# Reading the scan's decay from PSUM and forming the gate's product on GpSimd

## The chip, the cores and the metric

The kernel runs on one NeuronCore of a Trainium2 chip, in one launch. The metric is the device time of one execution in microseconds (us); the time of a kernel is the median of its runs. The core has five engines that each work through their own queue in order: TensorE (PE, matrix products into PSUM), VectorE (DVE), ScalarE (ACT), GpSimd (POOL) and SyncE (SP, which issues most DMAs). They wait for each other through semaphores.

## What is computed

Four residual layers work on 32 images of 192 channels and 56 x 56 pixels: agent attention, a bidirectional RWKV scan, a shifted depthwise 3 x 3 filter and a long convolution done through spectra. Each begins with a group norm. The change touches the second layer alone. With `xs` the normed images as 3136 pixels of 192 channels:

```python
k, v, r = xs @ Wk.T, xs @ Wv.T, xs @ Wr.T
real_w = -exp(w_decay)                       # one number per channel
x_fwd = wkv_scan(real_w, u, k, v)            # running sums over the pixels
x_bwd = flip(wkv_scan(real_w, u, flip(k), flip(v)))
h = sigmoid(r) * 0.5 * (x_fwd + x_bwd)
h = layernorm(h) * ln_g + ln_b               # over the channels
out = x + h @ Wo.T
```

`wkv_scan` keeps a numerator and a denominator per channel, multiplies both by `exp(real_w)` at every pixel and adds `exp(k) * v` and `exp(k)`; the present pixel enters with the weight `exp(u)`; the quotient is the result. The kernel keeps the two sums without the running maximum (a guarded version, `scan_guarded`, is there for inputs that need it, and is not entered here).

## The kernel before

`all_blocks` runs four stages one after another: `make_filter`, `attention`, `scan_pairs`, `channel_blocks`. The change is in `scan_pairs`.

**Tiles.** Two images are worked on at once, as a pair; there are 16 pairs. The 2 x 192 channels of a pair fill three tiles of 128 partitions: tile 0 holds channels 0 to 127 of the first image, tile 1 those of the second, and tile 2, the third tile, the remaining 64 of both. The 3136 pixels go in four pieces of 784 (`MC`), so an elementwise instruction is 128 x 784, and a matrix product fills two PSUM banks with 392 columns each (`HM`).

**Products.** `turned()` (L925) gives a PSUM tile of two banks out of a pool of four, which is all of PSUM (eight banks). Products for tiles 0 and 1 are made together by `_Pairs.outer` (L886 to L893): four matmuls of L890, then four of L893, into two PSUM tiles. Products for the third tile are made by `_Pairs.inner` (L895 to L903): two matmuls of L900, then four of L903, into one. The profile records each matmul twice, so a pair of tiles shows as 8 and 8, a third tile as 4 and 8.

**One step.** The loop at the end of `scan_pairs` runs over pairs and pieces. A full step does, for three different places in the data: `backwards` (the backward scan of one piece), `finish` (layer norm, output product and residual of the piece that `backwards` ended a step earlier), and `forwards` (the forward scan of a piece of the next pair). There are 60 full steps, four forward-only pieces ahead of them, and four steps without `forwards` at the end.

The lines of a step, by name:

- `normed` (L1110): ACT applies the group norm to the loaded `x`.
- `forwards`: the product with `Wk`; ACT takes the exponential, `ek` (L1159); the product with `Wv`; DVE multiplies it by `ek`, giving `bv` (L1164); then `scan`, `inverse` and `y = p * q` on DVE (L1174).
- `scan` (L1113 to L1132), once for `bv` (giving `p`) and once for `ek` (giving `q`): POOL copies the carry into the edge column (L1123), DVE runs the scan (L1128), POOL copies the last column out as the next carry (L1129), DVE adds the present pixel with its weight (L1130). Carries are named f and b for forward and backward, with 0 for p or 1 for q, and the tile: f11 is the forward carry of q in tile 1.
- `inverse` (L1135, L1136): ACT inverts the denominator through Ln and Exp.
- `backwards`: the product with `Wr`; ACT makes the gate `g` in three instructions (L1188, L1192, L1193); the scans; on DVE the quotient (L1196), its sum with the forward result (L1197) and the product with the gate (L1198).
- `finish`: the product of `h` with a centring matrix; ACT squares it (L1213); the mean over channels of the squares, a product for tiles 0 and 1 alone (two PSUM tiles, from `mean_w`); ACT forms the reciprocal deviation through Ln and Exp (L1222, L1223); two DMAs on ACT's queue bring it into the third tile's layout; the output product with `wog`; DVE scales it (L1236) and adds it to the image (L1239); ACT squares that for the next group norm (L1246).

**What sets the order.** The source order is only the input of a scheduler that runs when the program is built. It simulates the engines with costs of its own and picks, for every engine, a fixed order, and it places the waits. It treats two accesses of different engines to the same PSUM tile as ordered when they share a bank, whether or not they share columns. On the chip each engine takes its queue in that order.

The lines that a sentence does not say:

```python
def turned():
    ps = pp.tile([128, 2, BANK], F32, name="ps", tag="ps")
    return ps, ps[:, :, :HM], [ps[:, h, :HM] for h in range(2)]
...
nc.vector.tensor_tensor_scan(out, decay[:, of(t)].to_broadcast([128, MC]), data, at, ALU.mult, ALU.add)
nc.gpsimd.tensor_copy(at, z[:, last : last + 1])
nc.vector.scalar_tensor_tensor(before, src, c, before, ALU.mult, ALU.add)
```

`decay` is a tile of two columns in SBUF: one for tiles 0 and 1, one for the third. The scan reads one of them with step zero, 784 times.

Of the kernel before, what the change touches and what calls it, by code (L numbers as in the profile page):

```python
# [20 lines left out]
F32 = mybir.dt.float32  # L21
I32 = mybir.dt.int32
AF = mybir.ActivationFunctionType
ALU = mybir.AluOpType
AX = mybir.AxisListType
PSUM = bass.MemoryType.PSUM
# [10 lines left out]
MC = 784  # L37
NM = N // MC
HM = MC // 2
# [26 lines left out]
BANK = 512  # L66
# [840 lines left out]
def scan_pairs(ctx: ExitStack, tc: tile.TileContext, a, k, x1, st_a, st_c, x2, rs2, count):  # L907
# [5 lines left out]
    nc = tc.nc  # L913
# [2 lines left out]
    kp = ctx.enter_context(tc.tile_pool(name="s_k", bufs=3 * NM))  # L916
    wp = ctx.enter_context(tc.tile_pool(name="s_w", bufs=9))
    sp = ctx.enter_context(tc.tile_pool(name="s_s", bufs=2))
    pp = ctx.enter_context(tc.tile_pool(name="s_p", bufs=4, space=PSUM))
    pairs = _Pairs(nc)  # L920

    def small(name, shape):
        return cp.tile(shape, F32, name=name, tag=name)

    def turned():  # L925
        ps = pp.tile([128, 2, BANK], F32, name="ps", tag="ps")
        return ps, ps[:, :, :HM], [ps[:, h, :HM] for h in range(2)]

    def parts(t):
        return [t[:, h * HM : (h + 1) * HM] for h in range(2)]  # L930
# [21 lines left out]
    ps, _, _ = turned()  # L952
# [22 lines left out]
    decay, near, far = small("decay", [128, 2]), small("near", [128, 2]), small("far", [128, 2])  # L975
# [13 lines left out]
    nc.vector.tensor_tensor(near, near, z, ALU.mult)  # L989
    nc.vector.tensor_tensor(decay, near, far, ALU.add)  # L990

    eps = small("eps", [128, 1])
    nc.vector.memset(eps, 4.0 * LN_EPS)
    kept_a, kept_c = small("kept_a", [128, 2, NB // 2]), small("kept_c", [128, NB // 2])
# [5 lines left out]
    def of(t):  # L1000
        return slice(0, 1) if t < 2 else slice(1, 2)
# [111 lines left out]
    def scan(s, m, t, carry, rev):  # L1113

        b, e = s.bv[m][t], s.ek[m][t]
        c = eu[:, of(t)]
        got = []
        for i, src in enumerate((b, e)):
            z = wp.tile([128, MC + 1], F32, name="pq"[i], tag="pq", bufs=5)
            edge, last = (MC, 0) if rev else (0, MC)  # L1120
            out, before = (z[:, 0:MC], z[:, 1:]) if rev else (z[:, 1:], z[:, 0:MC])
            at = carry[t][i]
            nc.gpsimd.tensor_copy(z[:, edge : edge + 1], at)  # L1123
            if rev:
                out, data = out[:, ::-1], src[:, ::-1]
            else:
                data = src[:, :]
            nc.vector.tensor_tensor_scan(out, decay[:, of(t)].to_broadcast([128, MC]), data, at, ALU.mult, ALU.add)  # L1128
            nc.gpsimd.tensor_copy(at, z[:, last : last + 1])  # L1129
            nc.vector.scalar_tensor_tensor(before, src, c, before, ALU.mult, ALU.add)  # L1130
            got.append(before)
        return got  # L1132
# [12 lines left out]
    def forwards(s, m, behind=()):  # L1145
        s.ek[m] = [kp.tile([128, MC], F32, name="ek", tag="ek", bufs=3 * NM + 1) for _ in range(3)]
        s.bv[m] = [kp.tile([128, MC], F32, name="bv", tag="bv") for _ in range(3)]
        s.y[m] = [kp.tile([128, MC], F32, name="y", tag="y", bufs=3 * NM + 4) for _ in range(3)]
        xn = normed(s, m)
        for tiles in ((0, 1), (2,)):  # L1150
            for wt in (wk, wv):
                ps = [turned() for _ in tiles]
                if len(tiles) == 2:
                    pairs.outer(wt, [q[2] for q in ps], xn)
                else:
                    pairs.inner(wt, ps[0][2], xn)
                for t, (_, both, _) in zip(tiles, ps):
                    if wt is wk:
                        nc.scalar.activation(  # L1159
                            s.ek[m][t].rearrange("p (h n) -> p h n", h=2), both, AF.Exp,  # L1160
                            accum_out=s.seen[:, 0, 3 * m + t : 3 * m + t + 1],
                        )
                    else:
                        nc.vector.tensor_tensor(  # L1164
                            s.bv[m][t].rearrange("p (h n) -> p h n", h=2), both,
                            s.ek[m][t].rearrange("p (h n) -> p h n", h=2), ALU.mult,
                        )
                if wt is wk and tiles == (0, 1):
                    for later in behind:
                        later()  # L1170
            for t in tiles:
                num, den = scan(s, m, t, s.fore, False)
                inverse(s, den, m, t, 1)
                nc.vector.tensor_tensor(s.y[m][t], num, den, ALU.mult)  # L1174

    def backwards(s, m):

        xn = normed(s, m)
        h = s.y[m]
        for tiles in ((0, 1), (2,)):  # L1180
            ps = [turned() for _ in tiles]
            if len(tiles) == 2:
                pairs.outer(wr, [q[2] for q in ps], xn)
            else:
                pairs.inner(wr, ps[0][2], xn)
            for t, (_, both, _) in zip(tiles, ps):
                g = wp.tile([128, MC], F32, name="g", tag="t")
                nc.scalar.activation(  # L1188
                    g.rearrange("p (h n) -> p h n", h=2), both, AF.Exp, scale=-1.0,
                    accum_out=s.seen[:, 3, 3 * m + t : 3 * m + t + 1],  # L1190
                )
                nc.scalar.activation(g, g, AF.Ln, bias=1.0)  # L1192
                nc.scalar.activation(g, g, AF.Exp, scale=-1.0)  # L1193
                num, den = scan(s, m, t, s.back, True)
                inverse(s, den, m, t, 2)
                nc.vector.tensor_tensor(num, num, den, ALU.mult)  # L1196
                nc.vector.tensor_tensor(h[t], h[t], num, ALU.add)  # L1197
                nc.vector.tensor_tensor(h[t], h[t], g, ALU.mult)  # L1198
            yield

    def finish(s, m):

        h, xs = s.y[m], load(s.p, m)
        hs = [parts(t) for t in h]
        sq = [wp.tile([128, MC], F32, name="sq", tag="t") for _ in range(3)]
        for tiles in ((0, 1), (2,)):
            ps = [turned() for _ in tiles]
            if len(tiles) == 2:
                pairs.outer(centre, [q[2] for q in ps], hs)
            else:  # L1210
                pairs.inner(centre, ps[0][2], hs)
            for t, (_, both, _) in zip(tiles, ps):
                nc.scalar.activation(  # L1213
                    sq[t].rearrange("p (h n) -> p h n", h=2), both, AF.Square,
                    accum_out=s.seen[:, 4, 3 * m + t : 3 * m + t + 1],
                )
        sqs = [parts(t) for t in sq]
        pv = [turned() for _ in range(2)]
        pairs.outer(mean_w, [q[2] for q in pv], sqs)
        rds = [wp.tile([128, MC], F32, name="rd", tag="t") for _ in range(3)]  # L1220
        for t, (_, both, _) in enumerate(pv):
            nc.scalar.activation(rds[t].rearrange("p (h n) -> p h n", h=2), both, AF.Ln, bias=eps)  # L1222
            nc.scalar.activation(rds[t], rds[t], AF.Exp, scale=-0.5)  # L1223

        for t, r in enumerate((slice(0, 64), slice(64, 128))):
            nc.scalar.dma_start(out=rds[2][r], in_=rds[t][r])
        yield
        left = []
        for tiles in ((0, 1), (2,)):
            po = [turned() for _ in tiles]  # L1230
            if len(tiles) == 2:
                pairs.outer(wog, [q[2] for q in po], hs)
            else:
                pairs.inner(wog, po[0][2], hs)
            for t, (_, out, _) in zip(tiles, po):
                nc.vector.tensor_tensor(  # L1236
                    sq[t].rearrange("p (h n) -> p h n", h=2), out, rds[t].rearrange("p (h n) -> p h n", h=2), ALU.mult
                )
                nc.vector.scalar_tensor_tensor(  # L1239
                    xs[t], sq[t], cb[:, of(t)], xs[t], ALU.add, ALU.add, accum_out=s.sums[:, t, m : m + 1]  # L1240
                )
                if m == NM - 1:
                    nc.vector.tensor_scalar(s.away[:, t], s.sums[:, t, m : m + 1], -1.0 / MC, None, ALU.mult)

                def square(t=t):
                    nc.scalar.activation(  # L1246
                        sq[t], xs[t], AF.Square, bias=s.away[:, t], accum_out=s.squares[:, t, m : m + 1]
                    )

                left.append(square)  # L1250
        rows = slice(m * MC // S, (m + 1) * MC // S)
        for r, t, i, c in places:
            nc.sync.dma_start(out=x2[c, i, rows, s.p], in_=xs[t][r].rearrange("p (h w) -> p h w", w=S))
        yield left
# [19 lines left out]
    for m in range(NM):  # L1274
        forwards(s, m)
# [45 lines left out]
    ps, _, _ = turned()  # L1321
# [608 lines left out]
```

## Time and profile before

| What | Value |
|---|---|
| runs | 12221.74, 12241.55, 12216.5 us; median 12221.74 us |
| profiled execution, its own time | 12216.98 us |
| span of its trace | 12215.1 us |
| mean granted TensorE clock | 0.958 |
| busy over the span | PE 90%, DVE 88%, ACT 59%, POOL 28% |
| `scan_pairs`, from the first scan on | about 4997 to 8390 us, 3393 us |

The profile is of one execution. Times in a trace count from the start of its span; the execution's own time is 1.9 us more than the span. A line of a group names the source line, the engine, the operation, the tiles written and read, the shapes, how often it ran, its busy time in all, the mean of one in ns, and the engine's idle time just before it with what ended that. In a timeline the first two columns are the start and the time taken (a merged row covers several instructions), and an idle time stands in brackets. The instructions of an engine overlap a little at their ends, so the pitch from start to start is shorter than the duration.

### The profile page before, as it was taken

To read this page: it belongs to the slowest core of one execution; us is meant where nothing else is said; L and a number is where in the kernel's file an instruction comes from. 1 tells how busy PE (TensorE), PEld (TensorE's weight loads), DVE (VectorE), ACT (ScalarE), POOL (GpSimd) and SP (SyncE) were. 2 spreads that over 40 slices of the span, in tenths; PEclk is the share of its full clock that TensorE was granted. 3 is DMA by queue.
4 is the path that set the end of the run, shared out by engine and by line. 5 is a ranking of instruction groups with operands and counts; after the bars stand their busy time and mean duration, and the time that the engine had idled before them with its cause. 6 is when DMAs were issued, how large, how long until landed. Compare 5 with 4: busy or idle time off the path is not lost. (4 is left out here: it accounts for less than half of the span.)

```text
span 12215.1 us, 157485 instructions
## 1 busy us (share of the span) xinstructions
PE 11030.6 (90%) x57358; PEld 6623.6 (54%) x57358; DVE 10753.1 (88%) x14722; ACT 7146.9 (59%) x14690; POOL 3400.5 (28%) x2568
## 2 busy tenths in 40 slices
PE   6999999999999999688888888886999999999999
PEld 3555555555555555333333333333666666666666
DVE  6888888888888888799999999996888899898897
ACT  3555555555555555466666666665666666666665
POOL 0000000000000000455555555555343343343330
PEclk9999999999999999899999999997999999999999
DMA  2222222222222222243334334334333333333331
GB/s 70 57 57 57 59 58 64 59 59 59 63 61 57 57 57 49 73 103 96 97 101 104 93 97 104 98 96 100 71 68 64 67 70 64 67 70 64 67 69 32
DMA packets 1959211, 876.56 MB, mean 72 GB/s; under 512 B 1821153, under 2 KB 1858292, under 8 KB 1949292
## 3 DMA queue, kind: packets, MB, share of 16 engines
q1 hardware_dynamic: 1948188, 840.69, 30.1%
q10 hardware_dynamic: 10240, 25.70, 0.8%
q8 instruction: 458, 7.50, 0.3%
q14 instruction: 325, 2.66, 0.1%
HBM read 482.13 MB, written 319.29 MB: 66 GB/s over the span
## 5 line engine op out<-in xcount | busy, mean ns | idle before, releaser
L619 DVE SCALAR_TENSOR_TENSOR o<-v_a,att_w,o 128x896 f32<-128x896 f32 (+1 forms) x1024 | 1056.8, 1032 | 467.3 <-ACT v_a L593 337.3
L1142 POOL MEMSET f<- 128x1 f32 x96 | 8.9, 99 | 4769.6 <-DMA st_c<-st 4764.6
L1793 ACT COPY y<-ps 64x252 f32<-64x252 f32 (+1 forms) x2376 | 808.7, 340 | 797.3 <-PE ps L1787 767.6
L1626 POOL TENSOR_TENSOR smooth<-smooth,more 114x896 f32<-114x896 f32 x384 | 866.3, 2259 | 1200.7 <-ACT more L1625 1141.2
L1709 PE MATMUL ps<-fixed,real 84*84 84x112 f32 x6144 | 1093.6, 260 | 0.0
L1709 PE MATMUL ps<-fixed,imag 84*84 84x112 f32 x6144 | 1091.1, 259 | 0.0
L1717 ACT ACTIVATE z<-ps,rs 84x112 f32<-84x112 f32 x3072 | 816.7, 355 | 322.1 <-PE ps L1709 319.5
L1709 PEld LDWEIGHTS ps<-fixed,real 84*84 84x84 f32 x6144 | 790.2, 154 | 158.4 <-issue 129.4
L1135 ACT ACTIVATE q<-q 128x784 f32<-128x784 f32 x384 | 328.5, 855 | 812.4 <-DVE q L1130 641.2
L1709 PEld LDWEIGHTS ps<-fixed,imag 84*84 84x84 f32 x6144 | 765.8, 153 | 0.0
L890 PE MATMUL ps<-sq,fixed 128*128 128x392 f32 x512 | 298.9, 746 | 425.9 <-ACT sq L1213 425.9
L636 ACT ACTIVATE pr<-ps,low 98x896 f32<-98x896 f32 (+1 forms) x384 | 352.3, 918 | 559.9 <-DVE low L634 559.9
L724 PE MATMUL ps<-gq_a,xs_a 128*112 128x294 f32 x1792 | 619.1, 427 | 45.7 <-DVE pq L729 45.7
L1787 PE MATMUL ps<-fixed,padded 114*128 114x168 f32 x3072 | 527.6, 322 | 134.6 <-DVE x L1729 118.3
L619 DVE SCALAR_TENSOR_TENSOR o<-v_c,att_w,o 128x448 f32<-128x448 f32 (+1 forms) x1024 | 638.3, 623 | 6.0 <-ACT v_c L604 0.9
L632 PE MATMUL ps<-xs_a,gk_a 128*98 128x448 f32 (+1 forms) x1536 | 637.1, 495 | 0.0
L633 PE MATMUL ps<-xs_c,gk_c 125*98 125x448 f32 (+1 forms) x1536 | 631.6, 492 | 0.0
L1728 PE MATMUL ps<-z,fixed 84*114 84x448 f32 x1536 | 609.7, 539 | 0.4 <-ACT z L1717 0.4
L725 PE MATMUL ps<-gq_c,xs_c 125*112 125x294 f32 x1792 | 608.3, 421 | 0.0
L890 PE MATMUL ps<-x,weights 128*128 128x392 f32 x1536 | 574.0, 517 | 31.1 <-DVE bv L1164 14.2
L737 ACT ACTIVATE pq<-pq 112x1176 f32<-112x1176 f32 x224 | 265.4, 1185 | 553.0 <-DVE pq L729 430.1
L1787 PEld LDWEIGHTS ps<-fixed,padded 114*128 114x128 f32 x3072 | 473.6, 198 | 206.1 <-DVE x L1729 140.5
(372 smaller groups left out, 29249.8 us busy)
## 6 DMA issues: line engine op xcount, KB each, us to landing
x<-x SPq DMA_DIRECT2D x576, 392.0 KB
x<-x SPq DMA_DIRECT2D x512, 196.0 KB
x<-zeros SPq DMA_DIRECT2D x192, 399.0 KB
shifted<-x SPq DMA_DIRECT2D x192, 399.0 KB
x<-x SPq DMA_DIRECT2D x192, 399.0 KB
out_x<-x SPq DMA_DIRECT2D x384, 196.0 KB
x<-in_x SPq DMA_DIRECT2D x32, 1568.0 KB
x<-x SPq DMA_DIRECT2D x32, 1568.0 KB
```

What stands on the lines that cost most here:

```text
L619: nc.vector.scalar_tensor_tensor(dst, tap(i), dww[:, t, i : i + 1], dst, ALU.mult, ALU.add)
L632: mm(ps[P2, h, :n], g[:, cols], xs_a[j][:, px], start=True, stop=False)
L633: mm(ps[P2, h, :n], gk_c[0:KC, 2 * j + h, cols], xs_c[j][0:KC, px], start=False, stop=True)
L724: mm(ps[:SUB, i, :HA], xs_a[j][:, px], g, start=True, stop=False)
L725: mm(ps[:SUB, i, :HA], xs_c[j][0:KC, px], gq_c[0:KC, 2 * j + (q + i) // ns], start=False, stop=True)
L890: mm(out, aa, srcs[t][h], start=True, stop=False)
L1626: nc.gpsimd.tensor_tensor(y, y, more, ALU.add)
L1709: nc.tensor.matmul(ps[:84, i * 2 * S : (i + 1) * 2 * S], part[:, i0 + i].rearrange("p s u -> p (s u)"), f3[:, m, :], start=(m == 0), stop= ...
L1717: nc.scalar.activation(z[:, i0 + i].rearrange("p m w -> p (m w)"), ps[:84, i * 2 * S : (i + 1) * 2 * S], AF.Copy, scale=q.rs[:, i0 + i : i ...
L1728: nc.tensor.matmul(got, f4[:, m, :], z[:, i0 : i0 + n, m, :], start=(m == 0), stop=(m == 1))
L1787: nc.tensor.matmul(ps[:, g * 168 : (g + 1) * 168], flat[:, (g0 + g) * 128 : (g0 + g + 1) * 128], f1, start=True, stop=True)
L1793: nc.scalar.copy(y[64 * m : 64 * m + 64, 2 * g0 + i : 2 * (g0 + n) : 2], got[64 * i : 64 * i + 64, :, :, m, :])
```

## The change

A PSUM tile `own` of two banks is taken once and kept. All products for the third tile go there; the products for tiles 0 and 1 share the remaining three. The two columns of the decay are copied once into columns 392 and 393 of the first bank of `own`, behind the 392 that the products fill, and every scan reads them there. The product with the gate moves from DVE to POOL.

```diff
-    pp = ctx.enter_context(tc.tile_pool(name="s_p", bufs=4, space=PSUM))
+    pp = ctx.enter_context(tc.tile_pool(name="s_p", bufs=3, space=PSUM))
+    own = pp.tile([128, 2, BANK], F32, name="own", tag="own", bufs=1)
...
-    def turned():
-        ps = pp.tile([128, 2, BANK], F32, name="ps", tag="ps")
+    def turned(third=False):
+        ps = own if third else pp.tile([128, 2, BANK], F32, name="ps", tag="ps")
         return ps, ps[:, :, :HM], [ps[:, h, :HM] for h in range(2)]
...
+    pace = own[:, 0, HM : HM + 2]
+    nc.vector.tensor_copy(pace, decay)
...
-            nc.vector.tensor_tensor_scan(out, decay[:, of(t)].to_broadcast([128, MC]), data, at, ALU.mult, ALU.add)
+            nc.vector.tensor_tensor_scan(out, pace[:, of(t)].to_broadcast([128, MC]), data, at, ALU.mult, ALU.add)
...
-                ps = [turned() for _ in tiles]
+                ps = [turned(t == 2) for t in tiles]
...
-                nc.vector.tensor_tensor(h[t], h[t], g, ALU.mult)
+                nc.gpsimd.tensor_tensor(h[t], h[t], g, ALU.mult)
```

The edit of `turned(t == 2)` is made in `forwards`, `backwards` and twice in `finish`, so five products of a full step use `own`: those with `Wk`, `Wv`, `Wr`, the centring matrix and `wog`. In the changed file lines up to 920 keep their numbers; in `scan` and below they are higher by 5 (L1128 becomes L1133, L1198 becomes L1203).

More of the change, by code (lines that the diff above doesn't have):

```diff
@@ L1180, in backwards @@
         for tiles in ((0, 1), (2,)):
-            ps = [turned() for _ in tiles]
+            ps = [turned(t == 2) for t in tiles]
             if len(tiles) == 2:
@@ L1206, in finish @@
         for tiles in ((0, 1), (2,)):
-            ps = [turned() for _ in tiles]
+            ps = [turned(t == 2) for t in tiles]
             if len(tiles) == 2:
@@ L1229, in finish @@
         for tiles in ((0, 1), (2,)):
-            po = [turned() for _ in tiles]
+            po = [turned(t == 2) for t in tiles]
             if len(tiles) == 2:
```

## The prediction

> **What bounds the kernel now.** First the busy time of the scan stage (columns: stretch, length, PE, PEld, DVE, ACT, POOL, granted clock, DMA share, GB/s):
>
> ```profile
> 5083.00:8390.00 3307.00, 2745.99 (x10011) 1252.04 (x10011) 3217.21 (x3316) 2113.54 (x3631) 1941.04 (x1649) 0.92 0.39 98
> ```
>
> DVE is busy 3217 of 3307 us: it bounds this stage, and its 90 us of idle time make 1.4 us in each of 64 steps. A full step lasts 53.2 us (mean distance of the first L1196 of a step to the next one's), so DVE's work is 51.8. PE has 17% to spare. Second, the groups of the stage:
>
> ```profile
> L1129 POOL COPY f<-p 128x1 f32<-128x1 f32 x192 | 405.7, 2113 | 313.3 <-DVE p L1128 305.4
> ...
> L1128 DVE TENSOR_TENSOR_SCAN p<-decay,b,bv 128x784 f32<-128x784 f32 x192 | 354.6, 1847 | 0.0
> ...
> L1198 DVE TENSOR_TENSOR y<-y,g 128x784 f32<-128x784 f32 x191 | 183.4, 961 | 0.0
> ...
> L1164 DVE TENSOR_TENSOR bv<-ps,ek 128x784 f32<-128x784 f32 x192 | 180.6, 967 | 1.2 <-PE ps L893 1.2
> L1174 DVE TENSOR_TENSOR y<-p,q 128x784 f32<-128x784 f32 x192 | 180.2, 965 | 0.0
> ```
>
> L1198 is what leaves DVE. A copy of one column on POOL takes 2113 ns beside scans: it waits for DVE to let go. Third, timelines for pitches, of DVE, then of PE, and of PE after a pause (start, time, engine, line):
>
> ```profile
> 6491.14 3.60 DVE L1128 TENSOR_TENSOR_SCAN q<-decay,f,ek 128x784 f32<-128x784 f32 x2
> 6494.65 1.96 DVE L1130 SCALAR_TENSOR_TENSOR q<-ek,eu,q 128x784 f32<-128x784 f32 x2
> 6496.52 1.85 DVE L1164 TENSOR_TENSOR bv<-ps,ek 128x784 f32<-128x784 f32 x2
> 6498.29 3.59 DVE L1128 TENSOR_TENSOR_SCAN p<-decay,f,bv 128x784 f32<-128x784 f32 x2
> ```
> ```profile
> 6489.20 2.90 PE L890 MATMUL ps<-x,weights 128*128 128x392 f32 x8
> 6492.03 1.59 PE L893 MATMUL ps<-x,weights 64*128 64x392 f32 x8
> 6493.55 1.58 PE L900 MATMUL ps<-x,weights 128*128 128x392 f32 x4
> 6495.06 1.54 PE L903 MATMUL ps<-x,weights 128*64 128x392 f32 x8
> ```
> ```profile
> 5508.33 4.83 PE L890 MATMUL ps<-sq,fixed 128*128 128x392 f32 x8 [8.83 <-ACT sq L1213]
> 5513.09 1.59 PE L893 MATMUL ps<-sq,fixed 64*128 64x392 f32 x8
> ```
>
> From start to start a scan takes 1.76 us, L1130 0.94, a plain product 0.885, L1239 with its accumulator 1.03. On PE four L890 take 2.83, four L893 1.52, and a third tile's product 3.05 from its first start to its last end (the 302 such groups of the stage: median 3.051). After 8.83 us of idling the same four L890 take 4.76. I sorted all PE pauses of the stage by length: all 46 of 3 us and more were followed by such a slow start, of the pauses between 2 and 3 us most. So a pause of 3 us costs the next group about 1.9 us.
>
> **The change part by part.** *Gate product.* DVE loses 3 x 0.885 = 2.65 us a step. POOL gains three products. Nearest rows: L1619 (two operands, 928 columns, 1828 ns) and L1626:
>
> ```profile
> L1626 POOL TENSOR_TENSOR smooth<-smooth,more 114x896 f32<-114x896 f32 x382 | 861.9, 2259 | 1192.0 <-ACT more L1625 1141.2 <-ACT smooth L1622 36.3
> ```
>
> Scaled to 784 columns that is 1.54 to 1.98 us; I take 1.98. Beside L1626, DVE's L1696 (both operands in SBUF) averaged 1.47 us, away from it 0.65; L1694 (one operand in PSUM) 0.62 and 0.60. So a product on POOL can hold up DVE instructions with two SBUF operands, by up to 1.98 us each. In the built order the first of the three starts while DVE ends an L1130 and then waits for ACT anyway, the second starts ahead of a wait of DVE, and the third ahead of two L1164, which read PSUM. I take 0, and keep 0 to 5.9 us a step. Behind the products in POOL's queue stand column copies for scans; DVE needs those three or more instructions later. PE's centring product waits for the gate products, and comes to them 5 us after they end.
>
> *Scan from PSUM.* L1164 with a PSUM operand and L1174 without take 967 and 965 ns: I take 1.76 us unchanged; by these rows 768 scans differ by under 15 us either way. What POOL's copies gain (2113 ns down to perhaps 0.2) was hidden, since DVE does not wait for them in the trace.
>
> *The shared bank.* Here the change pays. The built program makes each product into `own` wait for the last scan ahead of it, and each scan for the last reader of `own` on ACT. In the old order these products took any free PSUM tile and DVE hardly waited. All of a full step's waits, with the times from the rows above (ACT: Ln or Exp 0.85, L1159 and L1213 0.8 and 0.1 for the accumulator, L1222 0.91; a handover 0.05):
>
> A, forward. The third tile's `Wk` product waits for scan f11. It starts cold, since PE has been out of work for 4 us, and ends after 5.0 us; `ek` on ACT ends at 5.95; PE meanwhile has other matmuls until 6.85; the `Wv` product then ends at 9.9, and DVE's bv follows at 10.0. Between f11 and that bv DVE has L1174, two L1130 and L1174: 3.65 us (in 28 of 64 steps about 4.0). Wait: 6.2 us on average.
>
> B, backward. The centring product waits for scan b11; cold, it ends at 5.0. ACT squares it at 5.45 to 6.35 (an inverse is ahead); four L893 end at 8.0; two Ln and two Exp run from 7.65 to 10.95; PE's third `Wr` product ends at 11.1 and `wog` for tile 1 at 13.4. DVE's L1236 of tile 1 stands ahead of scan b02 in its queue and so starts at 13.4, b02 at 14.25. DVE's work between is 8.3 us. Wait: 5.95 us.
>
> C. The third `wog` product waits for scan b12 (3.05 us and handovers, PE warm); DVE has 2.9 us. Wait: 0.35 us.
>
> D. Behind it, the next pair's `Wk` product, `ek` and `Wv` product end 9.1 us after b12; DVE reaches its bv at 6.85. Wait: 2.25 us.
>
> Together 14.75 us. A full step: 51.8 - 2.65 + 14.75 = 63.9 us, 10.7 more than 53.2; sixty make 642. The four last steps have B and C alone: 4 x (6.3 - 2.65) = 15. The four forward pieces ahead have A, an estimate of 4 x 5 = 20. Sum +677 us. On the profiled execution's 12216.98 us that is 12,894; the median of the runs is 5 us above that execution. I say 12,895. Outside the scan stage each engine's order is the same.
>
> PSUM is the place where a rule speaks against the change: the Trainium skill's "PSUM — Partial Sum Buffer", section "PSUM bank collisions raise a hardware error", says to guard by bank and quadrant and not by address, since two engines in one bank collide even at different columns. The trace of before can't show it; by that rule none of the waits A to D can be left out, and by the columns alone, which do not overlap, the sum would be the 170 us gain. The skill's "SBUF — State Buffer", section "Who interferes with whom", speaks for the change: a DVE instruction with one SBUF input does not contend with GpSimd. No row of before shows a scan with one; by the rule the copies of 2113 ns shrink.
>
> **The rivals.**
>
> *Warm PE, fewer waits.* If PE stays at full rate, A falls to 4.3 us (the product ends at 3.1, PE's other matmuls at 4.95, `Wv` at 8.0); if ACT has nothing ahead of the square in B, its chain is 3.05 + 0.9 + 1.5 + 3.05 + 2.25 and the handovers, 11.3, a wait of 3.9; D might vanish. 4.3 + 3.9 + 0.35 = 8.55 us, a step of 57.7: 60 x 4.5 + 4 x 1.6 + 4 x 4 = +292, 12,510. For it: the floor holds in any case; against it: the 46 cold starts.
>
> *POOL holds DVE up as well.* If one product in three meets a DVE instruction with two SBUF operands: 64 x 1.98 = 127 on top, 13,020; two, 13,150. For it: L1696's 1.47 us; against it: DVE waits just where the products run.
>
> *The scan holds POOL off as before*, the change not doing what it says: products then begin only between DVE instructions, and each can delay a scan by 1.98 us: up to 192 x 1.98 = 380 on top, 13,275. POOL's copies would stay near 2 us.
>
> *Faster.* If the handovers are hidden, because `own` is free again before DVE gets to the next scan or reader, DVE stays full and the stage loses 64 x 2.65 = 170 us: 12,047. It decides where the chain in A is shorter than DVE's 3.65 us. For it: DVE bounds the stage and loses work. Against it: two products and an `ek` in a row are 3.05 + 0.9 + 3.05 = 7.0 us at PE's best.
>
> **How the numbers follow.** Forecast 0.62; warm PE 0.20; POOL as well 0.10; scans hold POOL off 0.04; faster 0.04. The likeliest gives 12,895. The range reaches from the warm floor, 12,510, to 13,110, between POOL's one and two collisions. About 0.2% is what a measurement can tell from no change: faster 0.04, the same 0.01, slower 0.95.
>
> **What the next profile would show.** Right, if DVE's idle time in the scan stage is near 900 us against 90, ended by PE into `own` at bv (L1169, some 370 us) and by PE or ACT at L1241 (some 350), if the wait of PE for DVE scans at L900 is long, the granted clock in the stage falls below 0.92, L1203 stands on POOL at 1.5 to 2.3 us, scans stay at 1.83 us, and the column copies shrink to some 0.2 us beside scans. Wrong, if bv starts within a microsecond of DVE's previous instruction: then the shared bank does not cost what I say. Wrong in size, if third products after a pause take 3.05 us.

## The result, and the profile after

The changed kernel takes 12956.24 us (median of 4 runs, 12951.85 to 12963.59) beside 12223.63 us for the kernel before on the same chip: a ratio of 1.0595, 95% interval 1.0579 to 1.0611. It is slower by about 733 us. The profiled execution took 12951.85 us against 12216.98, 734.9 more, and its span is 12950.1 us at a mean granted clock of 0.946.

All of it lies in the scan stage. From the first scan to the end of the last, the stage lasted 3385.3 us before and 4128.0 now, 743 us more. First the busy times in nearly the same stretch as in the prediction (columns as there):

```profile
5083.00:9100.00 4017.00, 3009.41 (x10016) 1345.24 (x10012) 3119.89 (x3111) 2145.07 (x3620) 1308.58 (x1846) 0.89 0.32 81
```

DVE was busy for 3217 of 3307 us; now it is busy for 3120 of 4017. No engine is full any more, although the work is the same: that is what a row looks like when engines wait for each other in a ring. The granted clock fell from 0.92 to 0.89. Over exactly the stage, DVE's busy time went from 3297.6 to 3209.3 us and its idle time from 87.7 to 918.7. Second, DVE's groups in the stage, and where that idle time stands:

```profile
L1133 DVE TENSOR_TENSOR_SCAN p<-own,f,bv 128x784 f32<-128x784 f32 x192 | 354.4, 1846 | 2.2
...
L1179 DVE TENSOR_TENSOR y<-p,q 128x784 f32<-128x784 f32 x192 | 184.9, 963 | 228.6 <-ACT q L1141 228.6
...
L1201 DVE TENSOR_TENSOR p<-p,q 128x784 f32<-128x784 f32 x188 | 181.6, 966 | 186.3 <-ACT q L1141 186.3
L1169 DVE TENSOR_TENSOR bv<-ps,ek 128x784 f32<-128x784 f32 x128 | 118.9, 968 | 121.8 <-PE ps L893 121.8
L1241 DVE TENSOR_TENSOR sq<-ps,rd 128x784 f32<-128x784 f32 x122 | 118.8, 974 | 187.6 <-ACT rd L1228 106.8 <-PE ps L893 76.4 <-ACT x L1115 4.3
L1169 DVE TENSOR_TENSOR bv<-own,ek 128x784 f32<-128x784 f32 x64 | 62.4, 975 | 146.8 <-PE own L903 146.8
L1241 DVE TENSOR_TENSOR sq<-own,rd 128x784 f32<-128x784 f32 x61 | 59.5, 975 | 18.7 <-PE own L903 16.7
```

A scan takes as long from PSUM as from SBUF: 1846 ns here against 1835 for the same group before, and 1835 against 1840 over all 768. The six rows that follow hold 890 of the 919 us of idle time. Who starts the ring is in the table of waits:

```profile
PE own L900 <- DVE q L1133: 841.4, 183, 10.8
```

PE waits some 183 times, about three times a step, for a DVE scan before it may write the shared tile, 841 us in all. The kernel before has no such row. One such round on the timeline (start, time, engine, line; idle time in brackets):

```profile
6517.30 2.98 PE L900 MATMUL own<-x,weights 128*128 128x392 f32 x4 [4.77 <-DVE q L1133]
...
6521.85 0.82 ACT L1164 ACTIVATE ek<-own 128x784 f32<-128x784 f32 x1 [0.96 <-PE own L903]
...
6522.67 0.85 ACT L1141 ACTIVATE q<-q 128x784 f32<-128x784 f32 x1
...
6523.64 0.97 DVE L1179 TENSOR_TENSOR y<-p,q 128x784 f32<-128x784 f32 x1 [2.80 <-ACT q L1141]
...
6526.83 0.97 DVE L1169 TENSOR_TENSOR bv<-own,ek 128x784 f32<-128x784 f32 x1 [2.22 <-PE own L903]
```

Scan f11 runs from 6515.42 to 6517.24. PE, idle for 4.77 us by then, starts the third `Wk` product 0.06 us after its end, and slowly (2.98 us for the four records of L900, against 1.58 on a PE that has been working). ACT takes `ek` from it, and only behind that, in ACT's queue, comes the inverse (L1141) that DVE's L1179 waits for. DVE stops a second time at bv. 2.80 + 2.22 = 5.02 us are lost in this round.

The other two parts of the change, from the changed kernel's rows by line (min, median and max in ns):

```profile
L1134 POOL COPY f<-p x192: 185/185/197, 5015.7 to 9004.2; 128x1 f32<-128x1 f32 x192
L1134 POOL COPY f<-q x192: 777/840/1788, 5017.5 to 9006.0; 128x1 f32<-128x1 f32 x192
```
```profile
L1203 POOL TENSOR_TENSOR y<-y,g x192: 1838/1856/2606, 5135.4 to 9149.2; 128x784 f32<-128x784 f32 x192
```

The copy beside a scan, 2113 ns on average before, takes 185. The one of `q` stands beside L1135, which reads two SBUF operands, and takes 840 (median). The gate's product takes 1.86 us on GpSimd in the median and 2.08 on average: 63 of the 192, one a step, take over 2.3 us.

### The profile page after: what moved, and what is told of

Its sections match the earlier page's. It is cut to its first block, busy times and chain, and to the rows that moved or that the text cites. A ratio compares the mean times of both kernels' runs of the same rounds, so it can differ in the third digit from the quotient of the medians.

```text
span 12950.1 us, 157842 instructions
## 1 busy us (share of the span) xinstructions
PE 11301.1 (87%) x57358; PEld 6715.4 (52%) x57358; DVE 10653.8 (82%) x14531; ACT 7184.3 (55%) x14690; POOL 2749.9 (21%) x2760
## 5 line engine op out<-in xcount | busy, mean ns | idle before, releaser
L900 PE MATMUL own<-x,weights 128*128 128x392 f32 x768 | 386.4, 636 | 286.3 <-DVE q L1133 283.2
L900 PE MATMUL own<-y,fixed 128*128 128x392 f32 x256 | 189.1, 893 | 507.7 <-DVE q L1133 507.6
L1115 ACT ACTIVATE x<-x,nb,rs 128x784 f32<-128x784 f32 x384 | 396.5, 1034 | 340.9 <-DMA x<-x 337.6
```

## The experiments

Every kernel below computes the whole result. Stage times, busy and idle times are DVE's from the first scan to the end of the last. The kernel before took 12223.34 us (13 runs) beside `own_scan`, `own_only`, `gate` and `bank_gate`, 12225.38 (7 runs) beside `part_f`, `part_b`, `scan_part` and `three`, 12220.82 (14 runs) beside `bank_dve`, `mix` and `gate_third`, and 12223.29 (9 runs) beside `own_gate`.

### Which part of the change costs

`own_scan` is the changed kernel with the gate's product back on DVE:

```diff
-                nc.gpsimd.tensor_tensor(h[t], h[t], g, ALU.mult)
+                nc.vector.tensor_tensor(h[t], h[t], g, ALU.mult)
```

> The change without its part on GpSimd: the decay is read from the shared tile, the gate's product is back on DVE. Theory (the waits between the scans and the third-tile products, which share a bank, cost the time): the waits stay; three products of 0.885 us a step come back to DVE, and some of them fall into waits of DVE, so 12,950 to 13,130 us, DVE idle for 700 to 900 us in the scan stage. Rival (GpSimd's product holds DVE up by its lock on the shared port): the time goes back below 12,500 us.

It took 12952.16 us (12941.76 to 12963.69), ratio 1.0596 (1.0578 to 1.0613): the same as the changed kernel. DVE's busy time is 3361.1 us, 152 more than in the changed kernel, and its idle time 766.1, 153 less. The gate's product came out of idle time and went back into it. So it explains neither the loss nor a part of it.

`own_only` has the tile for third products and the three others, but each scan's decay in SBUF and the gate on DVE:

```diff
-    pace = own[:, 0, HM : HM + 2]
-    nc.vector.tensor_copy(pace, decay)
...
-            nc.vector.tensor_tensor_scan(out, pace[:, of(t)].to_broadcast([128, MC]), data, at, ALU.mult, ALU.add)
+            nc.vector.tensor_tensor_scan(out, decay[:, of(t)].to_broadcast([128, MC]), data, at, ALU.mult, ALU.add)
...
-                nc.gpsimd.tensor_tensor(h[t], h[t], g, ALU.mult)
+                nc.vector.tensor_tensor(h[t], h[t], g, ALU.mult)
```

> The third-tile products keep their one tile, but the decay is read from SBUF as before, and the gate's product is on DVE: no scan touches a bank that a product fills. Theory (the scans in the bank): the products no longer wait for scans; what is left is that the product with Wv waits for ek to be read, so 12,224 to 12,450 us and no wait of PE for a scan at L900. Rival (one tile for all third-tile products, and three for the rest, is what costs): 12,800 us or more.

12212.64 us (10 runs, 12203.76 to 12224.21), ratio 0.9993 (0.9983 to 1.0002). Five third products a step in one tile cost nothing. `own_scan` differs from it in the source of the scans' decay alone: 12952.16 - 12212.64 = 739.5 us. That settles which part costs: the scans' reads in the tile that PE writes.

`own_gate` completes the square. It is the changed kernel with the scans back in SBUF and the gate left on GpSimd, the first two hunks of the diff above.

> The changed kernel with one thing undone: every scan reads its decay from SBUF. It completes the square of scan source and gate engine on the tile for third products (SBUF and DVE 12,213; PSUM and DVE 12,952; PSUM and GpSimd 12,956). Theory: the scans in the shared bank are the whole loss, and the gate on GpSimd is worth a small loss here as it was on the old tiles (12,274: scans with two SBUF operands become longer by up to 1.9 us, DVE's idle time rises to some 165 us). So 12,240 to 12,310, with the mean of some scans above 2 us. Rival one: with the shared tile's other order the gate's product comes out ahead: under 12,200. Rival two: the gate's product needs the scan in PSUM, and every product locks a scan: 192 x 1.9 = 365 us against 170 saved, over 12,380.

12264.26 us (12256.37 to 12273.86), ratio 1.0034 (1.0021 to 1.0048): in the theory's range, and in neither rival's. Its sign, scans above 2 us on average, did not come: the longest group of scans averages 1865 ns. What grew is L1133 of `q` (1152 ns against 1018 in `own_only`) and the two products behind the inverse (1091 and 1085 against 967 and 964). In one table, all on the layout with a tile for third products:

| decay read from | gate on DVE | gate on GpSimd |
|---|---|---|
| SBUF | 12212.64 | 12264.26 |
| the shared PSUM tile | 12952.16 | 12956.24 |

Read down, the scans cost 740 or 692 us; read across, the gate's move is a loss of 52 us, or nothing. (The four stand beside runs of the kernel before whose medians agree within 0.4 us.)

### Why the gate's product gains nothing even by itself

`gate` is the kernel before with only the gate's product on GpSimd:

```diff
-                nc.vector.tensor_tensor(h[t], h[t], g, ALU.mult)
+                nc.gpsimd.tensor_tensor(h[t], h[t], g, ALU.mult)
```

> The part on GpSimd alone: the kernel before, with the gate's product on GpSimd; scans read the decay from SBUF. Theory: DVE loses 64 x 2.65 = 170 us of work, but a scan with two SBUF operands and the product on GpSimd shut each other out, so each of 192 products holds DVE up by up to 1.86 us (357 us): between 12,054 and 12,410 us, I expect some 12,250; column copies beside scans stay near 2 us. Rival (two SBUF operands of a scan don't matter): 12,060 us, with copies near 0.2 us.

12274.18 us (12269.2 to 12282.39), ratio 1.0043 (1.0026 to 1.006). DVE's busy time in the stage falls by 34 us instead of 170, and its idle time rises by 77. Two of its DVE groups:

```profile
L1128 DVE TENSOR_TENSOR_SCAN q<-decay,b,ek 128x784 f32<-128x784 f32 x192 | 441.0, 2297 | 0.0
...
L1128 DVE TENSOR_TENSOR_SCAN q<-decay,f,ek 128x784 f32<-128x784 f32 x192 | 349.2, 1845 | 90.5 <-ACT ek L1159 90.4
```

The backward scan of `q` grew from about 1.84 to 2.30 us on average, that is 192 x 0.46 = 89 us: 58 of the 192 take 3.38 us, the others 1.83. The timeline shows how, and also where the idle time comes from:

```profile
6500.77 3.46 POOL L1198 TENSOR_TENSOR y<-y,g 128x784 f32<-128x784 f32 x1
6502.44 3.44 DVE L1128 TENSOR_TENSOR_SCAN q<-decay,b,ek 128x784 f32<-128x784 f32 x1
...
6514.90 1.62 DVE L1239 SCALAR_TENSOR_TENSOR x<-sq,cb,x 128x784 f32<-128x784 f32 x1
...
6516.55 0.95 ACT L1246 ACTIVATE sq<-x,away 128x784 f32<-128x784 f32 x1 [0.98 <-DVE x L1239]
...
6517.50 0.80 ACT L1159 ACTIVATE ek<-ps 128x784 f32<-128x784 f32 x1
...
6518.43 1.85 DVE L1128 TENSOR_TENSOR_SCAN q<-decay,f,ek 128x784 f32<-128x784 f32 x1 [1.91 <-ACT ek L1159]
```

At 6502.44 a scan with two SBUF operands meets a running product, and the two take 3.44 and 3.46 us in place of 1.84 and 1.86. (The product began beside an L1130 and an L1196. If it had still to do its 1.86 us when the scan started, that explains both lengths; this is an estimate from the two ends, 6504.23 and 6505.88.) At 6514.90 an L1239 meets the third product of the step and takes 1.62 us instead of 1.03.

The wait of 1.91 us is not that delay: another step of this run has an L1239 of 1.02 us at 6353.73 and the same wait of 1.91. It is the order on ACT. Here `ek` (L1159) stands behind the third square (L1246), which waits for the third L1239. In the kernel before, `ek` stands ahead of that square:

```profile
6490.11 1.03 DVE L1239 SCALAR_TENSOR_TENSOR x<-sq,cb,x 128x784 f32<-128x784 f32 x1
...
6490.21 0.80 ACT L1159 ACTIVATE ek<-ps 128x784 f32<-128x784 f32 x1
...
6491.81 0.94 ACT L1246 ACTIVATE sq<-x,away 128x784 f32<-128x784 f32 x1
```

The scheduler picks this order when the program is built. It put `ek` behind the third square in 44 of some 60 full steps of `gate`, and in none before. In 30 of these 44 the scan waits, 57 us in all; in the other steps its wait went from 10 to 25 us. So it is mainly the growth of the scans and the changed order that the gate's product costs here. What it would bring with the old order on ACT was not measured.

### How much each wait is worth

`part_f` is the changed kernel with the decay of the two forward scans of tile 1 (f01, f11) in SBUF, which should remove wait A; `part_b` does the same to b01 and b11, for wait B; `scan_part` to all four.

```diff
-            nc.vector.tensor_tensor_scan(out, pace[:, of(t)].to_broadcast([128, MC]), data, at, ALU.mult, ALU.add)
+            nc.vector.tensor_tensor_scan(out, (decay if t == 1 and not rev else pace)[:, of(t)].to_broadcast([128, MC]), data, at, ALU.mult, ALU.add)
```

In `part_b` the condition is `t == 1 and rev`, in `scan_part` `t == 1`.

> As the changed kernel, but the forward scans of tile 1 (f01, f11) read the decay from SBUF. Theory (each scan in the bank that stands last ahead of a third-tile product costs a handover): the third product with Wk now waits for scan f10, and DVE has 6.35 us of work between that and bv instead of 3.65, so wait A falls from 6.2 to about 3.6 us; scan f11 moves ahead of the bv of the next pair and fills wait D (2.25 us). B stays. 60 x 4.8 = 290 us less than the changed kernel: 12,600 to 12,750 us, with the time under L1201 and L1241 on ACT and PE unchanged. Rival (the shared PSUM tile is slow for every scan alike, so two of twelve scans carry a sixth): 12,830 us.

> As the changed kernel, but the backward scans of tile 1 (b01, b11) read the decay from SBUF. Theory: the centring product waits for b10 instead of b11, and DVE has about 10.9 us of work up to the second L1241 against a chain of 13.4: wait B falls from 5.95 to about 2.5 us; the scan b01 and its L1135 move between f11 and bv, so A falls to about 3.6 us too; D stays. 60 x 6 = 360 us less: 12,520 to 12,680 us. Rival (all scans alike): 12,830 us.

> As the changed kernel, but all scans of tile 1 (f01, f11, b01, b11) read the decay from SBUF; eight of twelve scans still read PSUM and the gate's product stays on GpSimd. Theory: A has 9 us of DVE work against 10 (wait 1), B about 2.5 us, C and D are filled: 3.5 us in place of 14.75, so 60 x 11.2 = 670 us less, 12,240 to 12,400 us. Rival (all scans alike, four of twelve carry a third of 733 us): 12,710 us.

`part_f` took 12516.57 us (ratio 1.0237, 1.022 to 1.0254), `part_b` 12674.59 (1.0369, 1.0351 to 1.0386), `scan_part` 12473.9 (1.02, 1.0183 to 1.0217). Against the changed kernel these are 440, 282 and 482 us less. `part_b` came out as expected; `part_f` gained more and `scan_part` less than their ranges say, so both are misses. The idle time of DVE by group, in us, from the same view as above:

| DVE waits at | changed | part_f | part_b | scan_part |
|---|---|---|---|---|
| L1179 (A) | 228.6 | 0.1 | 230.9 | 3.1 |
| L1169 from `own` (A) | 146.8 | 59.7 | 5.3 | 35.0 |
| L1201 (B) | 186.3 | 127.1 | 49.4 | 117.0 |
| L1241 from `ps` (B) | 187.6 | 105.1 | 6.6 | 7.9 |
| L1169 from `ps` (D) | 121.8 | 0.0 | 116.3 | 0.0 |
| scan p of b | 4.1 | 13.6 | 9.0 | 135.1 |
| whole stage | 918.7 | 362.7 | 507.0 | 338.8 |

Taking f01 and f11 out of the tile takes the wait at L1179 away, and taking b01 and b11 out of it does the same to L1241 and most of L1201: each wait goes with the scans that the prediction named. But they do not add up. `part_f` also lost D and some of B, and `part_b` the half of A that stands at bv; `scan_part` has a new wait of 131 us, of a backward scan of `p` in PSUM for ACT's read of the gate (L1193) in the same tile. And GpSimd's product meets DVE again, in `part_f` this group:

```profile
L1133 DVE TENSOR_TENSOR_SCAN q<-decay,f,ek 128x784 f32<-128x784 f32 x64 | 187.0, 2921 | 13.8 <-ACT ek L1164 10.7
```

64 x (2.92 - 1.84) = 69 us. In `scan_part` L1244, L1201, L1202 and this scan grew in the same manner; in `part_b` the scans in SBUF did not (1875 and 1844 ns), but L1202 (1456 ns) and L1244 (1301) did. A caution belongs here: the program's scheduler picks the order anew for each variant. In the traces PE's products come nearly in the changed kernel's order in `own_scan` and `part_b`, but not in `part_f` and `scan_part`. So the table shows which scan causes which wait, and not the exact price of one.

### The decay in a bank of its own

PSUM has eight banks. If the decay gets one to itself, three tiles of two banks are left for all products, and no product shares a bank with a scan's operand. `bank_gate` does that to the kernel before and moves the gate to GpSimd; `bank_dve` is the same with the gate on DVE; `three` only takes the fourth tile away.

```diff
-    pp = ctx.enter_context(tc.tile_pool(name="s_p", bufs=4, space=PSUM))
+    pp = ctx.enter_context(tc.tile_pool(name="s_p", bufs=3, space=PSUM))
+    own = pp.tile([128, BANK], F32, name="own", tag="own", bufs=1)
...
+    pace = own[:, 0:2]
+    nc.vector.tensor_copy(pace, decay)
...
-            nc.vector.tensor_tensor_scan(out, decay[:, of(t)].to_broadcast([128, MC]), data, at, ALU.mult, ALU.add)
+            nc.vector.tensor_tensor_scan(out, pace[:, of(t)].to_broadcast([128, MC]), data, at, ALU.mult, ALU.add)
...
-                nc.vector.tensor_tensor(h[t], h[t], g, ALU.mult)
+                nc.gpsimd.tensor_tensor(h[t], h[t], g, ALU.mult)
```

> The decay in a PSUM bank of its own, that no product fills, three PSUM tiles for all products, the gate's product on GpSimd. Theory: the waits between scans and products are gone, scans leave GpSimd alone, DVE loses 170 us of work: 12,060 us, plus what the fourth PSUM tile was worth (0 to 140 us), so 12,060 to 12,200 us. Rival (scans from PSUM or the product on GpSimd cost the time): above 12,500 us.

> The kernel before with three PSUM tiles in place of four, nothing else changed. Theory for the kernel with the decay in a bank of its own (it lost 121 us where 100 or more were to be gained): the fourth PSUM tile was worth it, since DVE idled 304 us at bv for products; so the same waits appear here, 12,400 to 12,550 us. Rival (the loss there came from the scans in PSUM or the product on GpSimd): 12,220 to 12,280 us.

> The decay in a bank of its own, read by every scan; three two-bank tiles for all products; the gate's product back on DVE. It takes the earlier kernel with the gate on GpSimd (ratio 1.0107, 305 us of idle time of DVE at bv, waiting for a product) apart. Theory one: the order that the scheduler picks for three tiles, with scans that no longer hold POOL in its reckoning, is what costs; then this kernel too shows 200 us or more of idle time at bv (L1167) and takes 12,400 to 12,520, since DVE's 152 us come back on top of part of it. Theory two: the products on GpSimd shifted the order; then the idle time falls to that of the kernel with three tiles and nothing else (159 us) and the time to 12,270 to 12,330. If the scans' freedom from POOL's copies is worth nothing, this kernel cannot be under 12,224.

`bank_gate`: 12344.79 us, ratio 1.0107 (1.009 to 1.0124), a miss: I had hoped for a gain. `three`: 12300.71, ratio 1.0059 (1.0042 to 1.0076), between the two expectations. `bank_dve`: 12309.38, ratio 1.0074 (1.0061 to 1.0088), in the range of its second theory. The bv group of `bank_gate`, then that of `bank_dve`:

```profile
L1167 DVE TENSOR_TENSOR bv<-ps,ek 128x784 f32<-128x784 f32 x192 | 180.5, 968 | 304.3 <-PE ps L893 304.3
```
```profile
L1167 DVE TENSOR_TENSOR bv<-ps,ek 128x784 f32<-128x784 f32 x192 | 180.6, 968 | 176.8 <-PE ps L893 170.7 <-ACT x L1113 6.1
```

`bank_dve` and `three` differ by 9 us (their ratios by 0.0015, with intervals that overlap): 768 scans that read PSUM cost nothing measurable when no product is in their bank. The idle time stands elsewhere, at bv in `bank_dve` and at L1196 and the forward scan of `q` in `three` (87 and 72 us), so the two agree in the sum and not wait by wait. This is the other half of the proof that `own_only` began: neither a single tile for third products nor a scan from PSUM costs anything, only the two in one bank do. What `bank_dve` lacks is the fourth tile, some 75 us by `three`. With the gate on GpSimd on top, DVE's busy time falls by 102 us (3292.2 to 3190.3) and its idle time rises by 124, most of it at bv. `bank_gate` is even 35 us slower than `bank_dve`. Its L1242, two SBUF operands beside products of GpSimd, takes 1307 ns for 1026. And the order on ACT is again another: `ek` stands behind the third square in 58 of some 60 steps, in `bank_dve` ahead of it in 59. PE's `Wv` product for tiles 0 and 1 then waits 59 times, 134 us in all, for `ek`, in `bank_dve` once, and bv waits for that product. What order alone is worth was not tried.

### Two attempts at a faster version

`gate_third` is `own_only` with the third tile's gate product alone on GpSimd. `mix` also lets the forward scans of tile 0 read from the shared tile.

```diff
-            nc.vector.tensor_tensor_scan(out, decay[:, of(t)].to_broadcast([128, MC]), data, at, ALU.mult, ALU.add)
+            nc.vector.tensor_tensor_scan(out, (pace if t == 0 and not rev else decay)[:, of(t)].to_broadcast([128, MC]), data, at, ALU.mult, ALU.add)
...
-                nc.vector.tensor_tensor(h[t], h[t], g, ALU.mult)
+                (nc.gpsimd if t == 2 else nc.vector).tensor_tensor(h[t], h[t], g, ALU.mult)
```

> A candidate beside it: the tile for third products alone, every scan's decay in SBUF, only the third tile's gate product on GpSimd. 57 us less work on DVE. Theory: its GpSimd product meets one or two DVE instructions with two operands in SBUF, each of which becomes longer by up to 1.9 us, but DVE's idle time stays under 120: 12,190 to 12,240. Rival: it locks a scan as the three products do in the kernel with the gate alone (136 us of 170 lost): 12,210 to 12,260, with the mean of the b scans of q clearly above 1.85 us.

> A candidate. The tile for third products alone; only the forward scans of tile 0 read their decay there; only the third tile's gate product is on GpSimd. Theory: the scans of tile 0 lie where the shared tile is idle, so that they cost no wait; a third of the gate's products leaves DVE, 64 x 0.885 = 57 us less work; its GpSimd instruction meets mostly DVE instructions with an operand in PSUM. Then 12,170 to 12,230. Rival: the product locks a scan that still reads SBUF, or the forward scans of tile 0 do meet a product in the shared tile: 12,230 to 12,330, with scans above 1.85 us on average or an idle time over 150 us.

`gate_third` took 12252.14 us (ratio 1.0028, 1.0019 to 1.0038), 40 more than `own_only`: its time is in the rival's range, but the scans it named stayed at 1841 ns, so the rival's reason fails too. DVE's busy time did fall by 41 us; the wait of the forward scan of `q` for `ek` grew from 19 to 91 us, in the same place as in `gate` and with the same order on ACT (`ek` behind the third square in 44 steps). `mix` took 12390.25 us (ratio 1.0132, 1.0116 to 1.0147), above both expectations: PE's weight loads wait 61 times, 163 us in all, for a forward scan of tile 0 before a third product, and the scan of `q` waits 130 us for `ek` (both from 5083 us on). The assumption that the shared tile lies idle at that point was wrong. No version here beats the kernel before; `own_only` equals it.

## Why the prediction was right

The forecast was 12,895 us; the median is 12956.24, 61 above it and inside the range. The direction came from the right mechanism: PE and DVE wait for each other at the shared tile, after the scans that were named. By terms, in the stage, against 743 us measured and 677 forecast:

| Term | forecast, us | measured, us |
|---|---|---|
| wait A | 60 x 6.2 + 20 = 392 | 228.6 + 146.8 = 375 |
| wait B | 64 x 5.95 = 381 | 186.3 + 187.6 = 374 |
| wait C | 64 x 0.35 = 22 | 18.7 |
| wait D | 60 x 2.25 = 135 | 121.8 |
| other idle time of DVE | 0 | 29 |
| idle time that was there and goes | -84 | -87.7 |
| DVE's busy time | -64 x 2.65 = -170 | -88 |

*The waits* are right in size: 890 us in the four against 930. Where they stand was half right. I had put all of A at bv and all of B at L1241; the trace shows each split in two, with DVE first stopped at L1179 or L1201 by an inverse. ACT's queue explains it: the inverse stands behind the read of `own` that waits for PE, in A behind `ek`, in B behind the square, where I had put an inverse ahead of the square. The sum is the same, since the chain to bv ends when it ends, however the wait before it is divided.

*The gate's product* was right in its cost (1.86 us in the median and 2.08 on average, I took 1.98) and wrong in what it brings: -88, not -170. The step that failed is the one that cost everything beside the product at nothing. The durations of DVE's instructions in the stage fell by 162 us (3563.4 to 3401.2 in sum), which is 192 products of 0.96 less 22 us by which others became longer: L1244 is 1082 ns beside 1031, L1202 980 beside 968, and 15 short L1096 0.95 us beside 0.17. That is the small remainder of the rival "POOL holds DVE up", which had 127. The other 74 us are overlap: instructions of DVE that follow each other start before their predecessor has ended, and this sum of overlaps fell from 265.7 to 191.9 us. Some 15 of that go with the 192 instructions that left. The rest goes with the waits: DVE stands still 820 times in the stage, before 221 times (counting every break of more than 20 ns; half of the 820 are under 50 ns), and each further stop loses about 0.1 us of overlap. `own_scan`, with every instruction in place, shows it alone: 695 more stops, the same sum of durations, 64 us less overlap, 0.092 us each. This was the main shortfall: the sum was made with pitches of a stream without gaps, and gaps make each instruction behind them as long as its duration.

That the time came within 61 us has luck in it: the waits were put 40 us too high and the gain on DVE 82 too high, and 29 us of other idle time were left out, so the misses partly cancel.

*Cold PE* was right. The group of the third centring products shows it, on the page of the changed kernel:

```profile
L900 PE MATMUL own<-y,fixed 128*128 128x392 f32 x256 | 189.1, 893 | 507.7 <-DVE q L1133 507.6
```

This product follows a pause of about 8 us in each step (507.7 us over 64), and its matmuls are recorded at 893 ns on average, against 518 in the kernel before. From start to end a third product takes 4.65 us behind A's pauses and 5.24 behind B's (medians), where I had 5.0 for both, and 3.05 without a pause. The rival "warm PE" is out with it.

*The scan from PSUM* was right: 1840 ns on average before, 1835 after. Copies beside scans shrank to 185 ns as said for `p`; for `q` I had overlooked that the copy stands beside L1135. As to the Trainium skill's "SBUF — State Buffer", section "Who interferes with whom", which has DVE and GpSimd exclude each other from a shared port: the runs agree on both sides, with 185 ns beside scans that have one SBUF operand, and with 3.44 us for a scan with two beside a product.

*The bank rule.* The prediction weighed the rule of the Trainium skill's "PSUM — Partial Sum Buffer", section "PSUM bank collisions raise a hardware error", that guards go by bank. The program here orders by bank, and the runs show what that costs and that it is the bank which matters: 740 us with the decay in the products' bank, none measurable in another one. Whether reads and writes in one bank could have run side by side was not tried.

The rival "faster" needed the chain in A to be shorter than DVE's work. It is longer in the trace (5.02 us of waiting in the round shown). And none of the kernels without those waits shows the gain of 170 us: `gate` and `own_gate` are 51 and 41 us slower than the kernel before, and `bank_gate`, whose scans do read PSUM, is 35 slower than `bank_dve`. All three also have the changed order on ACT, so they don't show what the move would bring with the old one.

Left open: what fixes the price of a fourth PSUM tile at 75 us, what the gate's product on GpSimd is worth when ACT keeps its order, and how much of the differences among the `part` variants is due to the order picked for each.

## What to carry to other kernels

In a program that orders accesses by PSUM bank, as this one, a constant that one engine reads all the time makes the writers of its bank wait for that engine; give it a bank that nothing writes, and count what the bank's absence costs the products. Work taken off the bounding engine is a gain only if the engine that receives it does not hold the first one up, and only if what feeds the bounding engine can then come earlier. Where a scheduler picks the order, look whether the other engines' queues kept theirs: here a moved instruction changed ACT's. When you cost a wait, add the overlap that every stop loses to the wait itself.

## What was unexpected in the hardware

- A stop of DVE costs about 0.09 us more than the idle time that the profile shows, by the overlap that it breaks (695 stops, 64 us).
- A GpSimd product and a DVE scan with two SBUF operands do not share their time: in the round shown each took about 3.45 us, for 1.86 and 1.84 alone, and 58 of 192 backward scans of `q` took 3.38 us on average (`gate`).
- The fourth PSUM tile of two banks was worth 75 us (`three`) in a kernel whose DVE is 97% busy, and 0 when one of four is kept for third products alone (`own_only`).
